# Context columns made by VectorE's 32x32 transposes, with permuted query weights and 512-wide column tiles

## The chip, the cores and the metric

One core of a Trainium2 chip runs the whole program. The metric is the device time of one execution in microseconds, the median of several runs. TensorE (PE, with its weight loads as PEld), VectorE (DVE), ScalarE (ACT), GpSimd (POOL) and SyncE (SP, which here only issues transfers) each work through their own instruction queue in order and wait for one another by semaphores.

## The reference, cut to what matters

Eight examples, 64 slots of width 512 each, attend three times to a context of 1601 rows of width 512; then follow self-attention and a mixture of experts over the slots, which the change leaves alone. All is fp32.

```python
Pn = rmsnorm(P, input_norm_w)                 # P: 8 x 1601 x 512
k_proj, v_proj = Pn @ Wk.T, Pn @ Wv.T
for _ in range(3):
    sn = rmsnorm(slots, slot_norm_w)
    scores = einsum('bkd,bmd->bkm', sn @ Wq.T, k_proj) * SCALE
    attn = softmax(scores, axis=-2)           # over the 64 slots
    attn = attn / (sum(attn, axis=-1) + EPS)  # over the 1601 rows
    updates = einsum('bkm,bmd->bkd', attn, v_proj)
    slots = gru_cell(updates, slots, ...)
```

`rmsnorm` divides each context row by the root of its mean square, so that the sum of squares of every row is needed once.

## The kernel before, in words

The projections are folded: Wq and Wk become one matrix `wqk` (scaled by the slot norm's weights; the input norm's weights are applied to the query as `qscale`), and Wv is folded into the recurrent weights as `wvi`. So the scores are a product of the query with the raw context, and the context is needed in two layouts: with the 512 features on partitions ("columns", for the scores) and with the rows on partitions (for the weighted sum).

Two examples form a pair t, and there are four pairs. Each pair has three iterations, each of two halves: X makes the query and the scores and the softmax (`attend`, L335), Y makes the weighted sum and the recurrent cell (`update`, L423). Pairs 0 and 2 lead, pairs 1 and 3 trail by one iteration, so the halves of two pairs lie in turn (`stages`, L199 to L204).

In the first X of a pair, `prepare` (L270) makes the columns. The context comes in chunks of 1 MB, four rows of 512 features to a partition (`pn_X`), and a tail of 65 rows per example. For each 128 rows ACT squares the tile and sums the squares (L286, into `junk`), TensorE turns it in four 128x128 transposes (`transpose4`, L110, into PSUM tiles `tr_p`), and DVE and ACT in turn copy the result out (`evacuate`, L84 and L86) into a column tile `pT_a`. Column tiles hold 384 columns, the fourth 449. Each finished tile is also stored to DRAM (`kept`, issued by POOL at L294) and loaded again by the second and third iteration (`pT_X`). From the sums of squares, thirteen small DVE instructions (from L298 on) make the reciprocal roots `inv` and the roots `rms`, which the softmax uses.

`attend` turns the slots (`sT`), multiplies by `wqk` (`pq`), copies and turns the query (`qT`, DVE at L354) and multiplies it by the columns, group by group (`sc`, L364). ACT scales the scores out of PSUM (L370). Softmax then runs on blocks of 512 (L395 to L402 on DVE, exp on ACT), with POOL making row sums (`part`, L404 to L410). `update` reads the context rows (`pn_Y`), multiplies (`pu`, L433), and goes through the recurrent matmuls (L153) and the gate arithmetic on DVE and ACT (L459 to L470).

What sets the order: all context loads go through SP's queue in the order of the program (`queue`, L116). Chunks of rows have five slots (`nat`), column tiles five (`ctxT`), tails two; `pump` (L242) issues the next planned load as soon as a slot of its kind is counted free by `done` (L254). The other instructions are ordered per engine by a planner at compile time, which follows the program's priorities and its own estimates of when operands are ready; the order is then fixed. In the first X, the chunks are made inside `attend` through `start_group` (L489), between the folds of the value weights (`fold_values`). In the other first X's the whole of `prepare` stands ahead of `attend` in the program.

Of the kernel before, what the change touches and what calls it, by code (L numbers as in the profile page):

```python
# [9 lines left out]
F32 = mybir.dt.float32  # L10
I32 = mybir.dt.int32
AF = mybir.ActivationFunctionType
ALU = mybir.AluOpType
# [18 lines left out]
RSQRT_SEED = 0x5F3759DF  # L32


GROUPS = ((0, 384), (384, 768), (768, 1152), (1152, M))
GW = max(hi - lo for lo, hi in GROUPS)


@with_exitstack
def perceiver_kernel(  # L40
# [26 lines left out]
    def chunk(name, tag="w"):  # L67

        bufs, width = SLOTS[tag]
        return big.tile([P, width], F32, tag=tag, name=name, bufs=bufs)  # L70
# [4 lines left out]
    def bank(name, tag="ring"):  # L75
        return ps.tile([P, 512], F32, tag=tag, name=name)
# [3 lines left out]
    def evacuate(dst, src):  # L80

        copies[0] += 1
        if copies[0] % 2:
            nc.vector.tensor_copy(dst, src)  # L84
        else:
            nc.scalar.copy(dst, src)  # L86
# [19 lines left out]
    def transpose4(src, name, rows=P, tag="ring"):  # L106

        pt = bank(f"tr_{name}", tag).rearrange("p (c m) -> p c m", c=DC)
        for c in range(DC):
            nc.tensor.transpose(pt[:, c, :rows], src[:rows, ts(c, P)], ident[:rows, :rows])  # L110
        return pt[:, :, :rows]
# [4 lines left out]
    def queue(dst, src):  # L116

        return tc.keep_in_program_order(nc.sync.dma_start(dst, src))  # L118
# [11 lines left out]
        queue(wk_s[:, c, :], wk[ts(c, P), :])  # L130
    snw_s = const.tile([P, DC], F32, name="snw_s")
    inw_s = const.tile([P, DC], F32, name="inw_s")
    with nc.allow_non_contiguous_dma(reason="two short vectors onto partitions"):
        nc.gpsimd.dma_start(snw_s, snw.rearrange("(c p) -> p c", p=P))
        nc.gpsimd.dma_start(inw_s, inw.rearrange("(c p) -> p c", p=P))
    queue(xall, x.rearrange("(t p) d -> p t d", p=P))
    qscale = const.tile([P, DC], F32, name="qscale")
    nc.vector.tensor_scalar_mul(qscale, inw_s, float(D) ** -0.5)
    rw_s = const.tile([P, DC, E], F32, name="rw_s")
    nc.gpsimd.dma_start(rw_s, rw.rearrange("(c p) e -> p c e", p=P))  # L140

# [42 lines left out]

    mv0, r0 = layernorm(xall, "in", NPAIR)


    kept = [
        [
# [15 lines left out]

    tiles = {}
    held = {"nat": 0, "tail": 0, "ctxT": 0}
    plan = {"nat": [], "tail": [], "ctxT": []}  # L210
    BUFS = {"nat": SLOTS["nat"][0], "tail": 2, "ctxT": SLOTS["ctxT"][0]}
    for pos, (half, (t, it)) in enumerate(stages):
        if half == "Y" or it == 0:
            for k in range(3):
                for j in range(2):
                    plan["nat"].append((pos, ("row", half, t, it, j, k)))
            for j in range(2):
                plan["tail"].append((pos, ("row", half, t, it, j, 3)))
        if half == "X":
            for g in range(len(GROUPS)):  # L220
                for j in range(2):
                    plan["ctxT"].append((pos, ("col" if it else "made", half, t, it, j, g)))

    def load(key):
        kind, half, t, it, j, k = key
        b, name = 2 * t + j, f"{2 * t + j}_{k}_{half}{it}"
        if kind == "col":
            lo, hi = GROUPS[k]
            ct = chunk(f"pT_{name}", "ctxT")[:, : DC * (hi - lo)]
            queue(ct, kept[b][k])  # L230
            tiles[key] = ct.rearrange("p (c m) -> p c m", c=DC)
        elif k < 3:
            c = chunk(f"pn_{name}", "nat").rearrange("p (a f) -> p a f", a=4)
            src = ctxp[b, : MT * P, :].rearrange("(p i) d -> p i d", i=MT)
            queue(c, src[:, 4 * k : 4 * k + 4, :])
            tiles[key] = c
        else:
            tl = big.tile([P, D], F32, tag="tail", name=f"tail_{name}", bufs=BUFS["tail"])
            queue(tl[:TAIL], ctxp[b, MT * P :, :])
            tiles[key] = tl  # L240
# [13 lines left out]
    def done(tag, n=1):  # L254

        held[tag] -= n
        pump()

    def row_tile(half, t, it, j, i):

        c = tiles[("row", half, t, it, j, i // 4)]
        return c[:, i % 4, :] if i < MT else c[:TAIL]

    def row_used(i):
        if i % 4 == 3:
            done("nat")
        elif i == MT:
            done("tail")

    def prepare(t):  # L270

        ss = small.tile([P, NMT, 2], F32, tag="pss", name=f"pss_{t}", bufs=4)
        nc.gpsimd.memset(ss, 0.0)
        for g, (lo, hi) in enumerate(GROUPS):
            for j in range(2):
                b = 2 * t + j
                key = plan["ctxT"].pop(0)[1]
                assert key == ("made", "X", t, 0, j, g)
                held["ctxT"] += 1
                ct = chunk(f"pT_{b}_{g}_a", "ctxT")[:, : DC * (hi - lo)]  # L280
                c3 = ct.rearrange("p (c m) -> p c m", c=DC)
                for i in range(lo // P, (hi + P - 1) // P):
                    src = row_tile("X", t, 0, j, i)
                    k = src.shape[0]
                    junk = work.tile([P, D], F32, tag="junk", name=f"junk_{b}_{i}")
                    nc.scalar.activation(  # L286
                        junk[:k], src, AF.Square, accum_out=ss[:k, i, j : j + 1]
                    )
                    evacuate(
                        c3[:, :, i * P - lo : i * P - lo + k],  # L290
                        transpose4(src, f"p_{b}_{i}", k, "gate"),
                    )
                    row_used(i)
                nc.gpsimd.dma_start(kept[b][g], ct)  # L294
                tiles[key] = c3
            yield g
        v = small.tile([P, NMT, 2], F32, tag="pv", name=f"pv_{t}", bufs=2)
        nc.vector.tensor_scalar(v, ss, 1.0 / D, 1e-6, ALU.mult, ALU.add)  # L298
        ri = const.tile([P, NMT, 2], F32, name=f"inv_{t}")
        flat = "p i j -> p (i j)"  # L300
        rsqrt(ri.rearrange(flat), v.rearrange(flat), 2 * NMT, f"p_{t}")
        rms = const.tile([P, NMT, 2], F32, name=f"rms_{t}")
        nc.vector.tensor_mul(rms, v, ri)
        inv_of[t], rms_of[t] = ri, rms
# [17 lines left out]
        wih_2.append(w)  # L322
    wqk = chunk3("wqk")
    for dc in range(DC):
        if dc % 2:
            nc.vector.tensor_scalar_mul(wqk[:, dc, :], pw[dc], snw_s[:, dc : dc + 1])
        else:
            nc.scalar.mul(wqk[:, dc, :], pw[dc], snw_s[:, dc : dc + 1])
    b_h = work.tile([P, NMT * P], F32, tag="wide", name="b_h", bufs=3)[:, : 2 * D]
    nc.gpsimd.dma_start(b_h, bhh[: 2 * D].partition_broadcast(P))  # L330
    nc.vector.tensor_add(b_i[:, : 2 * D], b_i[:, : 2 * D], b_h)
# [3 lines left out]
    def attend(t, it, first=lambda g: None):  # L335
# [4 lines left out]
        nc.vector.tensor_copy(sT, transpose4(slots, f"s_{n}"))  # L340
        sT_of[t] = sT
        ss = small.tile([P, 1], F32, tag="sss", name=f"sss_{n}")
        junk = work.tile([P, D], F32, tag="junk", name=f"junk_{n}")
        nc.scalar.activation(junk, slots, AF.Square, accum_out=ss)
        nc.vector.tensor_scalar(ss, ss, 1.0 / D, 1e-6, ALU.mult, ALU.add)
        ri = small.tile([P, 1], F32, tag="sri", name=f"sri_{n}")

        pq = bank(f"pq_{n}")
        matmul4(pq, lambda c: sT[:, c, :], lambda c: wqk[:, c, :])
        q = work.tile([P, D], F32, tag="nat", name=f"q_{n}", bufs=2)  # L350
        nc.scalar.copy(q, pq)
        rsqrt(ri, ss, 1, f"s_{n}")
        qT = work.tile([P, DC, P], F32, tag="quT", name=f"qT_{n}", bufs=2)
# [4 lines left out]
        for g, (lo, hi) in enumerate(GROUPS):  # L358
            first(g)
            sc = bank(f"sc_{n}_{g}")[:, : hi - lo]  # L360
            cols = [tiles[("col" if it else "made", "X", t, it, j, g)] for j in range(2)]
            for c in range(DC):
                for j in range(2):
                    nc.tensor.matmul(  # L364
                        sc[j * S : (j + 1) * S, :],
                        lhsT=qT[:, c, ts(j, S)], rhs=cols[j][:, c, :],
                        start=c == 0, stop=c == DC - 1,
                    )
            done("ctxT", 2)
            nc.scalar.mul(raw[:, lo:hi], sc, ri)  # L370

        e = work.tile([P, NMT * P], F32, tag="wide", name=f"e_{n}", bufs=3)
# [50 lines left out]
    def update(t, it, att, banks=None):  # L423
# [6 lines left out]
        for i in range(NMT):  # L430
            k = P if i < MT else TAIL
            for j in range(2):
                nc.tensor.matmul(  # L433
                    pu[j * S : (j + 1) * S, :],
                    lhsT=e[:k, i, ts(j, S)], rhs=row_tile("Y", t, it, j, i),
                    start=i == 0, stop=i == MT,
                )
                row_used(i)
# [87 lines left out]
    NI = 8  # L526
    A = 4
    scale = float(HD) ** -0.5
    bq_n = work.tile([P, DX], F32, tag="junk", name="bq_n")[: 3 * HEADS, :P]
    bq_n = bq_n.rearrange("n (q c) -> n q c", q=4)  # L530
    for q in range(4):
        queue(bq_n[:, q, :], bqkv.rearrange("(n c) -> n c", c=HD))
# [199 lines left out]

    xbuf = dram.tile([NB * P, DX], F32, name="xbuf")
    back = dram.tile([TOP * NPAIR * P, D], F32, name="back")
    zeros = work.tile([P, DX], F32, tag="junk", name="zeros")
    nc.gpsimd.memset(zeros, 0.0)
    nc.gpsimd.memset(zeros[:, D : D + 1].bitcast(I32), TOP * NPAIR * P)
    tc.keep_in_program_order(nc.gpsimd.dma_start(
# [306 lines left out]
```

## Time and profile before

| what | value |
| --- | --- |
| device time, median of 3 runs | 1056.72 us (1051.85 to 1061.62) |
| the profiled execution: device time, span | 1067.05 us, 1065.3 us |
| mean granted TensorE clock | 0.969 |
| context chunks `pn_X` loaded by SP | 24 of 1 MB |
| column tiles stored, and loaded again | 32, 64 |
| DMA, mean over the span | 223 GB/s |

A line of groups has the source line, the engine, the operation, the tiles written and read, the partitions and elements, the number of instructions; then their busy time, the mean time of one in ns; then the idle time of the engine just before them and what ended most of it. A line of a stretch of time has busy times and instruction counts of the engines in it. Overlapping instructions of one engine count once in busy times.

### The profile page before, as it was taken

What the parts mean: (1) busy time and instruction counts of PE and PEld (TensorE: products, weight loads), DVE (VectorE), ACT (ScalarE), POOL (GpSimd) and SP (SyncE); (2) the same over time, 40 slices, a digit from 0 to 9 for tenths busy, and PEclk for the clock granted to TensorE, in tenths of its full rate; (3) what the DMA queues carried; (4) which work ended last, traced back from release to release, by engine and by line L of the source; (5) the groups of instructions that cost most, each with busy time, mean ns of one, the idle gap of its engine ahead of it and who ended that gap; (6) DMA issues with size and microseconds to landing.
All of it is one profiled execution on the core that took longest, in us unless ns stands there. A gap on an engine that the chain in (4) does not pass through costs nothing. (4 is left out here: it accounts for less than half of the span.)

```text
span 1065.3 us, 11266 instructions
## 1 busy us (share of the span) xinstructions
PE 971.7 (91%) x4081; PEld 461.3 (43%) x4081; DVE 428.6 (40%) x1059; ACT 246.7 (23%) x530; POOL 198.0 (19%) x295
## 2 busy tenths in 40 slices
PE   6899989899989997999898899899998988899994
PEld 3454354334433444444543344333443464675441
DVE  3224155532544347522554224452451445542223
ACT  1652552110211524205521001110110111211220
POOL 2003013300133004300132100330051211031221
PEclk9999999999999998999899999999999969999998
DMA  9946678864656647845787564596191300039943
GB/s 344 400 135 274 249 296 347 317 255 168 246 232 263 246 136 270 316 151 214 306 336 270 223 247 186 197 357 247 59 348 40 129 2 0 1 134 309 371 158 136
DMA packets 62425, 237.41 MB, mean 223 GB/s; under 512 B 5870, under 2 KB 20222, under 8 KB 50080
## 3 DMA queue, kind: packets, MB, share of 16 engines
q1 hardware_dynamic: 52576, 195.44, 48.6%
q0 software_dynamic: 8640, 39.14, 9.4%
q10 hardware_dynamic: 1152, 2.10, 0.5%
q8 instruction: 33, 0.54, 0.2%
q14 instruction: 24, 0.20, 0.0%
HBM read 201.22 MB, written 36.48 MB: 223 GB/s over the span
## 5 line engine op out<-in xcount | busy, mean ns | idle before, releaser
L433 PE MATMUL pu<-pn_Y,e 128*64 128x512 f32 x576 | 144.1, 609 | 5.7 <-DMA pn_Y<-in_ctxp 5.7
L364 PE MATMUL sc<-pT_X,qT 128*64 128x384 f32 (+1 forms) x512 | 102.4, 505 | 11.7 <-DMA pT_X<-kept 7.4
L404 POOL TENSOR_TENSOR raw<-e,rms 128x512 f32<-128x512 f32 (+1 forms) x48 | 44.8, 936 | 275.4 <-DVE sm L400 153.1
L433 PEld LDWEIGHTS pu<-pn_Y,e 128*64 128x64 f32 x576 | 42.3, 139 | 95.7 <-issue 79.6
L286 ACT ACTIVATE junk<-pn_X 128x512 f32<-128x512 f32 x96 | 60.4, 629 | 40.9 <-DMA pn_X<-in_ctxp 38.6
L364 PEld LDWEIGHTS sc<-pT_X,qT 128*64 128x64 f32 x512 | 38.1, 136 | 70.2 <-issue 47.8
L110 PE MATMUL tr_p<-ident,pn_X 128*128 128x128 f32 x384 | 53.4, 290 | 14.0 <-DMA pn_X<-in_ctxp 8.8
L395 DVE TENSOR_REDUCE mx<-tr_e 128x8 f32<-128x512 f32 (+1 forms) x48 | 26.9, 581 | 97.4 <-PE tr_e L384 97.3
L294 POOL DMA_DIRECT2D kept<-pT_a x32 | 17.4, 545 | 214.3 <-ACT r L467 66.3
L84 DVE COPY pT_a<-tr_p 128x512 f32<-128x512 f32 x52 | 34.7, 685 | 53.1 <-PE tr_p L110 31.8
L110 PEld LDWEIGHTS tr_p<-ident,pn_X 128*128 128x128 f32 x384 | 44.4, 147 | 26.9 <-issue 14.6
L370 ACT ACTIVATE raw<-sc,sri 128x384 f32<-128x384 f32 (+1 forms) x48 | 28.6, 596 | 107.8 <-PE sc L364 107.6
L153 PE MATMUL pq<-wqk,sT 128*128 128x512 f32 x96 | 48.0, 646 | 4.9 <-DVE sT L340 3.9
L153 PE MATMUL pr<-wvi,uT 128*128 128x512 f32 x96 | 45.5, 617 | 4.1 <-DVE uT L450 3.9
L398 ACT ACTIVATE e<-e 128x512 f32<-128x512 f32 (+1 forms) x48 | 25.8, 547 | 98.9 <-DVE e L397 98.8
L364 PE MATMUL sc<-pT_a,qT 128*64 128x384 f32 (+1 forms) x256 | 46.2, 503 | 2.4 <-DVE qT L354 2.4
L153 PE MATMUL pr<-whh,sT 128*128 128x512 f32 x96 | 48.1, 612 | 0.0
L153 PE MATMUL pqkv<-wqkv,haT 128*128 128x512 f32 x96 | 44.2, 618 | 1.4 <-ACT haT L549 1.4
L153 PE MATMUL pz<-whh,sT 128*128 128x512 f32 x96 | 44.7, 597 | 0.0
L153 PE MATMUL pab<-up_b,xT 128*128 128x512 f32 x96 | 43.2, 594 | 0.8 <-ACT xT L86 0.7
L153 PE MATMUL phn<-whh,sT 128*128 128x512 f32 x96 | 43.5, 592 | 0.0
L153 PE MATMUL pz<-wvi,uT 128*128 128x512 f32 x96 | 43.2, 592 | 0.0
(240 smaller groups left out, 1348.1 us busy)
## 6 DMA issues: line engine op xcount, KB each, us to landing
pn_Y<-in_ctxp SPq DMA_DIRECT2D x72, 1024.0 KB
pT_X<-kept SPq DMA_DIRECT2D x48, 768.0 KB
pn_X<-in_ctxp SPq DMA_DIRECT2D x24, 1024.0 KB
kept<-pT_a POOLq DMA_DIRECT2D x24, 768.0 KB, 8.6
pT_X<-kept SPq DMA_DIRECT2D x16, 898.0 KB
up_b<-in_w SPq DMA_DIRECT2D x24, 512.0 KB
kept<-pT_a POOLq DMA_DIRECT2D x8, 898.0 KB, 10.1
dn_b<-in_w SPq DMA_DIRECT2D x12, 512.0 KB
```

What stands on the lines that cost most here:

```text
L84: nc.vector.tensor_copy(dst, src)
L110: nc.tensor.transpose(pt[:, c, :rows], src[:rows, ts(c, P)], ident[:rows, :rows])
L153: nc.tensor.matmul(dst, lhsT=lhsT(c), rhs=rhs(c), start=start and c == 0, stop=stop and c == DC - 1,)
L286: nc.scalar.activation(junk[:k], src, AF.Square, accum_out=ss[:k, i, j : j + 1])
L294: nc.gpsimd.dma_start(kept[b][g], ct)
L364: nc.tensor.matmul(sc[j * S : (j + 1) * S, :], lhsT=qT[:, c, ts(j, S)], rhs=cols[j][:, c, :], start=c == 0, stop=c == DC - 1,)
L370: nc.scalar.mul(raw[:, lo:hi], sc, ri)
L395: nc.vector.reduce_max(mxr, rows3(pt), axis=AX.X)
L398: nc.scalar.activation(ee, ee, AF.Exp)
L404: nc.gpsimd.tensor_mul(rows3(prod), ee, wide(rms))
L433: nc.tensor.matmul(pu[j * S : (j + 1) * S, :], lhsT=e[:k, i, ts(j, S)], rhs=row_tile("Y", t, it, j, i), start=i == 0, stop=i == MT,)
```

## The change

The chunk loads of the first pass put the data so that DVE's 32x32 transposes are enough. A chunk is now 512 consecutive rows. Partition quadrant a (32 partitions) receives features 128a to 128a+127 of all 512 rows, in four transfers per chunk, one for each quadrant, in runs of 128 floats. Each partition then holds 16 runs of 128 features. Four DVE stream transposes of 128x512 turn every 32x32 block in place of its quadrant, straight from the chunk to the column tile. A feature that was on partition p of feature chunk c is now somewhere else, in blocks of 32: so `wqk`'s columns are written permuted (`by_block`), and the input norm's weights are loaded a second time in that order (`inw_b`) for `qscale`. Column tiles hold 512 columns; the tail of 65 rows has column tiles of its own (`tailT`, two slots), and is still turned by TensorE after POOL has permuted its features.

The sums of squares change with the layout. ACT squares the whole chunk in place after the transposes (128x2048), POOL adds 128 features down to 32 in two instructions (1024 and 512 elements), DVE reduces the 32. A row's sum then lies in four parts on four quadrants; TensorE adds these with a constant matrix (`fold`), four small matmuls for each pair, and DVE copies the result. The chunk's slot is released after the reduction. The scores read the columns with a pattern of 32-element blocks. The tile `junk` is gone; three other uses of it move to other tiles (`q`, `part`, and for the zeros stored to `xbuf` a weight slot).

```diff
-GROUPS = ((0, 384), (384, 768), (768, 1152), (1152, M))
-GW = max(hi - lo for lo, hi in GROUPS)
+KT = 4
+NK = MT // KT
+GW = KT * P
+Q = 32
+GROUPS = tuple((lo, min(lo + GW, M)) for lo in range(0, M, GW))
...
+        for a in range(P // Q):
+            nc.gpsimd.dma_start(
+                inw_b[ts(a, Q)], inw[ts(a, P)].rearrange("(b c) -> c b", c=Q)
+            )
...
-    nc.vector.tensor_scalar_mul(qscale, inw_s, float(D) ** -0.5)
+    nc.vector.tensor_scalar_mul(qscale, inw_b, float(D) ** -0.5)
...
+    def by_block(v):
+        return v.rearrange("p (a b c) -> p b a c", a=P // Q, c=Q)
...
+    BUFS = {"nat": SLOTS["nat"][0], "tail": 2, "ctxT": SLOTS["ctxT"][0], "tailT": 2}
...
+    def by_chunk(ct, g):
+        if g < NK:
+            return ct.rearrange("p (n b r) -> p b n r", b=DC, r=Q)
+        return ct.rearrange("p (b r) -> p b r", b=DC)
...
-        elif k < 3:
-            c = chunk(f"pn_{name}", "nat").rearrange("p (a f) -> p a f", a=4)
-            src = ctxp[b, : MT * P, :].rearrange("(p i) d -> p i d", i=MT)
-            queue(c, src[:, 4 * k : 4 * k + 4, :])
+        elif k < NK:
+            c = chunk(f"pn_{name}", "nat")
+            src = ctxp[b, ts(k, GW), :]
+            if half == "Y":
+                c = c.rearrange("p (i d) -> p i d", i=KT)
+                queue(c, src.rearrange("(p i) d -> p i d", i=KT))
+            else:
+                src = src.rearrange("(q r i) d -> r i q d", q=P // Q, r=Q)
+                for a in (0, 2, 1, 3):
+                    dst = c[ts(a, Q)].rearrange("r (i q d) -> r i q d", i=KT, d=P)
+                    queue(dst, src[:, :, :, ts(a, P)])
...
     def prepare(t):
-        ss = small.tile([P, NMT, 2], F32, tag="pss", name=f"pss_{t}", bufs=4)
+        ss = small.tile([P, NK, 2, KT, P // Q], F32, tag="pss", name=f"pss_{t}", bufs=1)
...
-                for i in range(lo // P, (hi + P - 1) // P):
-                    src = row_tile("X", t, 0, j, i)
-                    k = src.shape[0]
-                    junk = work.tile([P, D], F32, tag="junk", name=f"junk_{b}_{i}")
-                    nc.scalar.activation(
-                        junk[:k], src, AF.Square, accum_out=ss[:k, i, j : j + 1]
+                if g < NK:
+                    for i in range(KT):
+                        nc.vector.transpose(ct[:, ts(i, D)], src[:, ts(i, D)])
+                    nc.scalar.activation(src, src, AF.Square)
+                    sq = src.rearrange("p (n d) -> p n d", d=P)
+                    nc.gpsimd.tensor_add(sq[:, :, :64], sq[:, :, :64], sq[:, :, 64:])
+                    nc.gpsimd.tensor_add(sq[:, :, :32], sq[:, :, :32], sq[:, :, 32:64])
+                    nc.vector.reduce_sum(
+                        ss[:, g, j].rearrange("p i q -> p (i q)"), sq[:, :, :32], axis=AX.X
                     )
-                    evacuate(
-                        c3[:, :, i * P - lo : i * P - lo + k],
-                        transpose4(src, f"p_{b}_{i}", k, "gate"),
+                else:
+                    src = src[:TAIL]
+                    blocks = work.tile([P, D], F32, tag="nat", name=f"tailb_{b}", bufs=2)[:TAIL]
+                    nc.gpsimd.tensor_copy(
+                        blocks.rearrange("p (b a c) -> p b a c", b=DC, c=Q), by_block(src)
                     )
-                    row_used(i)
+                    nc.scalar.activation(src, src, AF.Square, accum_out=v[:TAIL, MT, j : j + 1])
+                    evacuate(tiles[key], transpose4(blocks, f"p_{b}", TAIL, "gate"))
                 nc.gpsimd.dma_start(kept[b][g], ct)
+                done("nat" if g < NK else "tail")
             yield g
+        ps4 = bank(f"pss_{t}", "gate")[:, : 2 * MT]
+        for q in range(P // Q):
+            nc.tensor.matmul(
+                ps4[ts(q, Q)], lhsT=fold, rhs=ss[:, :, :, :, q].rearrange("p k j i -> p (k j) i"),
+                start=True, stop=True,
+            )
+        nc.vector.tensor_copy(
+            v[:, :MT].rearrange("p (k i) j -> p k j i", k=NK),
+            ps4.rearrange("p (k j i) -> p k j i", k=NK, j=2),
+        )
...
     for dc in range(DC):
+        src, dst = by_block(pw[dc]), wqk[:, dc, :].rearrange("p (b a c) -> p b a c", b=DC, c=Q)
...
-                        lhsT=qT[:, c, ts(j, S)], rhs=cols[j][:, c, :],
+                        lhsT=qT[:, c, ts(j, S)], rhs=cols[j][:, c],
...
-            done("ctxT", 2)
+            done("ctxT" if g < NK else "tailT", 2)
...
-    zeros = work.tile([P, DX], F32, tag="junk", name="zeros")
+    zeros = chunk("zeros")[:, :DX]
```

## The prediction

> **What bounds the kernel now.** I read the page's first two parts, then the groups, then the same 197 us of the trace twice: busy times of the four stretches in which the context columns are made, once for all instructions and once for the transposes' tile `tr_p` alone. The page first, then a groups answer:
>
> ```profile
> PE 971.7 (91%) x4081; PEld 461.3 (43%) x4081; DVE 428.6 (40%) x1059; ACT 246.7 (23%) x530; POOL 198.0 (19%) x295
> ...
> L110 PE MATMUL tr_p<-ident,pn_X 128*128 128x128 f32 x384 | 53.4, 290 | 14.0 <-DMA pn_X<-in_ctxp 8.8 <-DVE pT_a L84 2.9 <-ACT pT_a L86 1.9
> L86 ACT COPY pT_a<-tr_p 128x512 f32<-128x512 f32 (+1 forms) x52 | 28.4, 554 | 32.1 <-PE tr_p L110 12.4 <-PE sc L364 11.6 <-DVE pT_a L84 7.3
> L84 DVE COPY pT_a<-tr_p 128x512 f32<-128x512 f32 x52 | 34.7, 685 | 53.1 <-PE tr_p L110 31.8 <-PE sc L364 16.6 <-ACT pT_a L86 4.7
> L643 DVE STREAM_TRANSPOSE on<-oT 128x512 f32<-128x512 f32 x4 | 2.7, 695 | 0.0
> ```
>
> TensorE is the bound: 91% busy, the next engine 40%. 53.4 us of it are the transposes that the change removes; the last line is the price of their replacement. The four stretches, all instructions, then `tr_p` alone:
>
> ```profile
> 24.00:86.00 62.00, 58.45 (x256) 32.52 (x257) 16.23 (x41) 33.55 (x80) 4.28 (x8) 0.97 0.75 289
> 124.00:165.00 41.00, 35.31 (x194) 21.03 (x193) 19.44 (x63) 21.47 (x52) 3.80 (x7) 1.00 0.62 243
> 380.00:437.00 57.00, 49.90 (x277) 27.94 (x276) 30.28 (x75) 21.14 (x47) 14.87 (x22) 0.91 0.72 253
> 506.00:543.00 37.00, 32.72 (x191) 20.84 (x190) 15.83 (x57) 17.94 (x41) 4.33 (x8) 0.91 0.82 317
> ```
>
> ```profile
> 24.00:86.00 62.00, 13.85 (x104) 12.30 (x104) 8.88 (x13) 7.16 (x13) 0.97 0.75 289
> 124.00:165.00 41.00, 12.27 (x104) 10.96 (x104) 8.56 (x13) 6.75 (x13) 1.00 0.62 243
> 380.00:437.00 57.00, 15.51 (x104) 11.88 (x104) 8.71 (x13) 7.06 (x13) 0.91 0.72 253
> 506.00:543.00 37.00, 13.11 (x104) 11.63 (x104) 8.56 (x13) 7.11 (x13) 0.91 0.82 317
> ```
>
> Columns after the stretch and its length: PE, PEld, DVE, ACT (in the first table POOL too), clock, DMA share, GB/s. The transposes take 12 to 16 us of each stretch, and PE idles only 3 to 7 us there: PE time removed is time of the stretch, if nothing else is late.
>
> **The parts, from rows.** *PE, removed:* 384 transposes, 53.4 us; the 32 of the two tails per pair stay. With them go waits of up to 14.0 us. *PE, added:* four folds of four small matmuls; a fp32 matmul is two records (the row sums `rs`, 12 in the code, are recorded 24 times), so 32 records at 46 ns (L624: 11.7/256) to 192 ns (L440: 4.6/24), 1.5 to 6.1 us; I take 3. *Scores:* before, 768 records. On PE's timeline 32 of 384 columns take 5.38 us, 168 ns each; 28 of these with 16 of 449 take 7.92 us, so a 449 takes 201 ns. After: 576 of 512 columns at 224 ns (168 scaled) to 250 ns (L433: 144.1/576), 192 of 65 at 46 ns (L624) to 139 ns (53.4/384). Change: 576 x (56 to 82) - 192 x 201 + 192 x (46 to 139) = +2.5 to +35 us; I take 3, since the same line scaled and the row of like size are nearest. That the column operand now comes in blocks of 32 elements has no row on PE; DVE's and ACT's block-wise copies (L638, 411 and 375 ns for 256) cost no more than plain ones (L447, L448: 483 and 474), so 0.
>
> *DVE:* 96 transposes x 0.695 = 66.7 us and 24 row reductions x 0.672 (L399's median) = 16.1 us come; all 52 copies (34.7 us) go and 4 of the tails' eight come back at some 0.4: +50 us, 12.5 a stretch. *ACT:* squares and their accumulator reads (60.4 + 18.0 us) and 48 of 52 copies (27) go; 24 squares of 2048 come, 1.6 us each by the slope from 256 to 512 elements (474 to 630 ns) to 2.5 us as four of 0.63: at 2.0, some -57 us. *POOL:* 24 x two adds of 1024 and 512 elements; 128, 256 and 512 take 0.45, 0.74 and 1.04 us (medians of L410, L406, L404), so 1.6 to 2.1 and 1.04: +70 us, 17 a stretch. ACT and POOL have room: the busiest stretch has 21 and 15 us of 57.
>
> *DMA:* each context megabyte of the first pass comes as four transfers onto 32 partitions in 512-byte runs, not as one in 8 KB runs. SP issues 72 more at 0.33 us, 24 us of an idle queue. At full share the trace moves 412 GB/s in 8 KB runs (162 to 177 us), and 368 GB/s in the experts' 1 and 2 KB runs (970 to 1000 us); 512 bytes are not shown. Bounds per megabyte: 2.5 us at 412, 5.7 us if a packet costs the same whatever its size (half of 368). I take the middle, 4.1: +1.6 us on 24 loads, 38 us. Room: unused DMA share in the four stretches is 62x0.25 + 41x0.38 + 57x0.28 + 37x0.18 = 54 us. It fits on average, but each load lands later.
>
> The Trainium skill speaks against this part (SBUF — State Buffer, section "Door 1: The DMA port swizzle"): 32 partitions reach 8 of 16 ports, 189 GB/s at 1 MiB against 328. As an estimate from its ratio, a megabyte would take 4.4 us, and the 24 loads 45 us more instead of 38. No transfer of before shows it.
>
> *At nothing:* four more short loads for `inw_b` on POOL at 0.82 us each delay its other loads by 3.3 us; the first read of these is at 23.9 us. The zeros in a weight slot that comes free only with the last update (829 us) are needed at 947. `junk` in place: ACT's own order. Six column tiles in five slots, where there were eight in five, can only shorten the 7.4 us that scores wait for `pT_X`; not counted.
>
> **What is kept of it on the path, by stretch.**
> First: SP has 12 transfers, not 3, ahead of wih_1; six chunks at +1.6 us land up to 10 us later. DVE's `wqk` (L326, at 30.75 us) stands behind context copies already and will stand behind transposes that wait for a slower load; behind it PE waits for `sT`. Of 13.85 I keep 7.
> Second and fourth: from 135.5 us, and the same after 507, PE ran 60 transposes while nothing else was released; DVE was busy 2.0 of 25 us just before (100 to 125), so columns can be made then, under the update's matmuls. I keep 12.3 + 13.1 + their waits for `pn_X` (2.4 + 1.9) = 29.7.
> Third: DVE runs almost without a gap from 395.8 to 417.7, softmax and column copies mixed, and `sT` of the next query (413.0 us) stands behind them. DVE's extra 12.3 us lie in just this queue. Of 15.5 and some 4.6 us of waits for copies I keep 20.1 - 12.3 = 7.8.
> Together 44.5. Off: folds 3, scores 3, and the new wait. The sum of squares of the last chunk now goes transposes, square (2.0), adds (2.9), reduction (0.7), fold: 5.6 us in which PE's fold, if it stands ahead of scores or `tr_e`, holds all behind it. Scores cover it in part; I take a quarter, 1.4 x 4 = 5.6. **Sum: 33 us saved.** The profiled execution took 1067.05 us (span 1065.3), 1.0% above the median of 1056.72; subtracted from that: **1024 us**.
>
> New waits and what stands behind them: DVE's reduction waits for POOL, and behind it stand `upd`, `uT`, `qT` and the gate arithmetic, for which PE waits; ACT's square waits for four transposes, with exp and tanh behind it; POOL's adds wait for ACT, with `kept` stores and the row sums behind.
>
> **Rivals.**
> *All of it is kept* (1000 us or less): DVE finds gaps everywhere and the tail hides; 53.4 + 14.0 - 6 = 61, so 996. For: DVE 40%. Against: third stretch.
> *Given back, no change* (about 1056): late context transfers and DVE's queue take PE's place in all four. At 5.7 us a megabyte six loads need 34 us, of stretches 37 to 62 us long that PE would leave 12 us shorter. For: DMA share 0.72 to 0.82 in the last two. Against: loads are issued 20 to 35 us ahead (347 and 476 us). Here belongs that PE work leaves without the program getting shorter.
> *Slower* (1076): DVE's in-order queue. Were each reduction to stand right behind its own transposes, DVE would stand still 2.0 + 2.9 = 4.9 us for each of 24 chunks, 118 us, beside waits for the slower loads. Where less than 28% of this (33/118) reaches PE the change still wins; at 45%, 53 us, it is 20 us slower. For: ACT, whose queue holds the squares now, waited 38.6 us for `pn_X`, where little depended on it; on DVE much does. The two engines also hinder each other: L406 on POOL takes 717, 744 (median) and 1726 ns. Against: order in the program is arranged by expected readiness; `wqk` and the copies of before are interleaved, not in the order written.
>
> **How the numbers follow.** Forecast 0.46 (1008 to 1045); all kept 0.13; given back 0.14; slower 0.27, of it a few hundredths for transfers alone. Within 1% (10.6 us) is about what a measurement of this kernel can't tell from no change: its three runs span 1051.85 to 1061.62. Faster by more: 0.46 + 0.13 = 0.59; same 0.14; slower 0.27. The range reaches from the upper part of "all kept" (1000) to a slower case of +22 us (1079).
>
> **What would show it.** Right: `tr_p` down to 32 records and PE near 925 us busy; 96 DVE stream transposes near 0.7 us; DVE near 480, ACT near 190, POOL near 270 us; PE's idle time in the stretches not above 30 us; the third gaining least. Wrong: DVE waiting tens of us for POOL sums or for `pn_X`; PE waiting for `qT`, `uT`, `pT_a` or the fold; a megabyte of 512-byte runs above 5 us; 65-column scores near 139 ns; transposes from SBUF slowed by POOL beside them.

## The result, and the profile after

The changed kernel takes **1150.51 us** (median; 1147.5 to 1153.92) against 1059.17 us of the kernel before in the same comparison: a ratio of 1.089, interval 1.082 to 1.096. It is slower by 91 us. The forecast was 1024 us.

The first part of the page of the changed kernel and two rows of its second part (busy tenths of PE, and the clock granted to it, in 40 slices of the span):

```profile
PE 941.2 (82%) x3729; PEld 418.2 (36%) x3729; DVE 475.1 (41%) x1135; ACT 198.0 (17%) x314; POOL 292.2 (25%) x360
...
PE   5399935789988994599828889988998888898994
...
PEclk9599976999999997799859999999998899999998
```

TensorE is still the busiest engine, but it now idles 1152.1 - 941.2 = 211 us of the span (94 before), and its clock falls where it idles. The groups of the same page that stand where the transposes and their copies stood:

```profile
L330 DVE STREAM_TRANSPOSE pT_a<-pn_X 128x512 f32<-128x512 f32 x96 | 59.9, 679 | 18.4 <-PE sc L425 16.4
L333 POOL TENSOR_TENSOR pn_X<-pn_X 128x1024 f32<-128x1024 f32 x24 | 56.5, 2355 | 40.5 <-ACT pn_X L331 35.6
L331 ACT ACTIVATE pn_X<-pn_X 128x2048 f32<-128x2048 f32 x24 | 45.8, 1908 | 105.4 <-DVE pT_a L330 105.3
...
L335 DVE TENSOR_REDUCE pss<-pn_X 128x16 f32<-128x512 f32 x24 | 16.4, 683 | 97.8 <-POOL pn_X L334 97.8
...
L113 PE MATMUL tr_p<-ident,tailb 65*128 65x65 f32 x32 | 5.2, 329 | 56.8 <-POOL tailb L341 56.8
```

The new work costs about what it was priced at (the second number after the bar is the mean in ns); only GpSimd's adds are longer. What was not priced is the third number, the idle time in front of it: VectorE stands 97.8 us for GpSimd's sums, ScalarE 105 us for VectorE's transposes, and TensorE 56.8 us for the permuted copy of the tail.

Where in the program is the time lost? TensorE turns the update (`tr_u`) at the same points of the work in both kernels. I cut both spans there: the stretches of one row hold the same work. Columns as before (stretch, length, PE, PEld, DVE, ACT, POOL busy, clock, DMA share, GB/s). The kernel before, the second, fourth and fifth of six stretches:

```profile
124.00:218.00 94.00, 82.38 (x395) 41.49 (x393) 48.80 (x125) 30.28 (x68) 24.25 (x34) 1.00 0.74 294
...
331.00:461.00 130.00, 122.25 (x504) 56.93 (x505) 58.48 (x138) 41.35 (x96) 24.59 (x35) 0.96 0.65 243
461.00:597.00 136.00, 121.94 (x504) 57.10 (x502) 58.02 (x143) 41.52 (x95) 25.48 (x35) 0.96 0.66 257
```

The changed kernel, the same three:

```profile
136.00:259.00 123.00, 78.95 (x312) 33.15 (x310) 60.77 (x144) 26.23 (x37) 47.48 (x49) 0.83 0.74 262
...
375.00:520.00 145.00, 111.36 (x413) 44.93 (x413) 72.76 (x157) 28.83 (x42) 46.15 (x49) 0.88 0.62 191
520.00:676.00 156.00, 115.90 (x416) 47.20 (x414) 68.84 (x162) 28.42 (x40) 48.97 (x49) 0.87 0.74 242
```

They last 29, 15 and 20 us longer; the first stretch (0 to 124, now 0 to 136) 12 us, the third 3, the rest 8. So most of the loss, 76 of 87 us of span, lies where columns are made. In the stretch of 123 us TensorE has 83 instructions less, yet is busy only 3.4 us less, with the clock at 0.83 there and 1.00 before, and idles 44 us instead of 12.

The timeline of that stretch shows how. VectorE of the changed kernel (start, length, instruction, and in brackets the idle time before it and what ended it):

```profile
159.90 0.69 DVE L335 TENSOR_REDUCE pss<-pn_X 128x16 f32<-128x512 f32 x1 [5.28 <-POOL pn_X L334]
160.50 2.48 DVE L330 STREAM_TRANSPOSE pT_a<-pn_X 128x512 f32<-128x512 f32 x4
168.84 0.69 DVE L335 TENSOR_REDUCE pss<-pn_X 128x16 f32<-128x512 f32 x1 [5.85 <-POOL pn_X L334]
169.44 2.48 DVE L330 STREAM_TRANSPOSE pT_a<-pn_X 128x512 f32<-128x512 f32 x4
177.77 0.69 DVE L335 TENSOR_REDUCE pss<-pn_X 128x16 f32<-128x512 f32 x1 [5.85 <-POOL pn_X L334]
```

Each reduction stands right behind the transposes of its own chunk, and the next chunk's transposes behind that (in the whole span VectorE waits so 20 times for 24 chunks): 2.48 us of transposes, 5.85 of standing, 0.69 of reduction, 8.9 us per chunk, from one start to the next, of which VectorE works 3.2. TensorE beside it:

```profile
148.36 0.60 PE L113 MATMUL tr_s<-ident,slots 128*128 128x128 f32 x4
149.90 3.70 PE L161 MATMUL pq<-wqk,sT 128*128 128x512 f32 x8 [0.94 <-DVE sT L402]
178.34 1.25 PE L113 MATMUL tr_p<-ident,tailb 65*128 65x65 f32 x8 [24.74 <-POOL tailb L341]
184.20 1.11 PE L113 MATMUL tr_q<-ident,q 128*128 128x128 f32 x4 [4.61 <-ACT q L412]
```

Behind the query's `pq` stand the tail's transposes. GpSimd permutes the tail at 177.68, behind the adds of the fourth chunk, so TensorE does nothing for 24.7 us; then `q` comes late, because ScalarE's copy of it (183.57) stands behind the square of one more chunk (180.88).

### The profile page after: what moved, and what is told of

Same layout as the page of the kernel before. It is cut to its first block, busy times and chain, and to the rows that moved or that the text cites. A ratio compares the mean times of both kernels' runs of the same rounds, so it can differ in the third digit from the quotient of the medians.

```text
span 1152.1 us, 10618 instructions
## 1 busy us (share of the span) xinstructions
PE 941.2 (82%) x3729; PEld 418.2 (36%) x3729; DVE 475.1 (41%) x1135; ACT 198.0 (17%) x314; POOL 292.2 (25%) x360
## 5 line engine op out<-in xcount | busy, mean ns | idle before, releaser
L425 PE MATMUL sc<-pT_X,qT 128*64 128x512 f32 (+1 forms) x512 | 98.3, 512 | 6.4 <-DVE qT L415 4.4
L161 PE MATMUL pq<-wqk,sT 128*128 128x512 f32 x96 | 55.5, 732 | 35.7 <-DVE sT L402 20.8
L330 DVE STREAM_TRANSPOSE pT_a<-pn_X 128x512 f32<-128x512 f32 x96 | 59.9, 679 | 18.4 <-PE sc L425 16.4
L333 POOL TENSOR_TENSOR pn_X<-pn_X 128x1024 f32<-128x1024 f32 x24 | 56.5, 2355 | 40.5 <-ACT pn_X L331 35.6
L331 ACT ACTIVATE pn_X<-pn_X 128x2048 f32<-128x2048 f32 x24 | 45.8, 1908 | 105.4 <-DVE pT_a L330 105.3
L335 DVE TENSOR_REDUCE pss<-pn_X 128x16 f32<-128x512 f32 x24 | 16.4, 683 | 97.8 <-POOL pn_X L334 97.8
L425 PE MATMUL sc<-pT_a,qT 128*64 128x512 f32 (+1 forms) x256 | 51.4, 543 | 2.4 <-DVE sss L407 1.6
L113 PE MATMUL tr_p<-ident,tailb 65*128 65x65 f32 x32 | 5.2, 329 | 56.8 <-POOL tailb L341 56.8
L431 ACT ACTIVATE raw<-sc,sri 128x512 f32<-128x512 f32 (+1 forms) x48 | 27.6, 595 | 125.8 <-PE sc L425 101.9
L161 PEld LDWEIGHTS pq<-wqk,sT 128*128 128x128 f32 x96 | 22.0, 239 | 66.1 <-issue 29.1
L161 PE MATMUL pz<-whh,sT 128*128 128x512 f32 x96 | 44.5, 594 | 0.0
```

The lines of the kernel that those rows point to most:

```text
L161: nc.tensor.matmul(dst, lhsT=lhsT(c), rhs=rhs(c), start=start and c == 0, stop=stop and c == DC - 1,)
L330: nc.vector.transpose(ct[:, ts(i, D)], src[:, ts(i, D)])
L331: nc.scalar.activation(src, src, AF.Square)
L333: nc.gpsimd.tensor_add(sq[:, :, :64], sq[:, :, :64], sq[:, :, 64:])
L335: nc.vector.reduce_sum(ss[:, g, j].rearrange("p i q -> p (i q)"), sq[:, :, :32], axis=AX.X)
L425: nc.tensor.matmul(sc[j * S : (j + 1) * S, :], lhsT=qT[:, c, ts(j, S)], rhs=cols[j][:, c], start=c == 0, stop=c == DC - 1,)
```

## The experiments

**Undoing the standing in the queues, one at a time.** `e1_order` moves each reduction two chunks later in VectorE's order:

```diff
+LAG = 2
...
-                    nc.vector.reduce_sum(
-                        ss[:, g, j].rearrange("p i q -> p (i q)"), sq[:, :, :32], axis=AX.X
-                    )
+                    late.append((g, j, sq))
+                    if len(late) > LAG:
+                        reduce_one()
```

> Edit: each chunk's reduction is put on DVE's queue behind the transposes of the second chunk after it; all the same instructions. Theory A (DVE stands behind each reduction for ACT's square and POOL's adds, 97.8 us in all, so that a chunk costs 8.9 us in series): DVE's wait for POOL falls below 30 us, the tail's copy on POOL is reached earlier, and the time falls from 1150 to 1040 to 1080. Theory B (PE's wait for the tail's permuting copy on POOL, 56.8 us, is its own fault): POOL's work is the same, 3.6 us a chunk with the copy in the same place behind four of them, PE still waits 40 us or more: 1120 to 1150. Theory C (the 512-byte loads arrive too slowly): chunks come no faster, 1130 to 1150.

`e2_tail` lets four loads with runs of 128 bytes permute the tail, in place of GpSimd's `tailb`; `e5_order_tail` does both; `e12_order_tailact` moves the reductions and has ScalarE make the copy of the tail:

```diff
-                    nc.gpsimd.tensor_copy(
+                    nc.scalar.copy(
```

> Edit: the tail of 65 rows is permuted by its load (four transfers in 128-byte runs) instead of by a copy on POOL; nothing else. Theory B: PE's 56.8 us of waiting for the copy go and the time falls by 40 to 57, to 1093 to 1110. Theory A: PE waits for DVE's columns and for the query's copies in DVE's queue instead, the time falls by 20 at most, 1130 to 1150. Theory C: as A.

> Both remedies at once: each reduction two chunks later in VectorE's order, and the tail's features permuted by four loads with runs of 128 bytes instead of GpSimd's copy. Queue theory (the time is lost where VectorE stands for GpSimd's sums and TensorE stands for the tail's permuted copy): alone they gave 23 and 6 us; the waits they remove are 83 of 98 us and 57 us, so together, when neither can hide behind the other, 40 to 60 us less than the changed kernel, 1090 to 1110 us. Load theory (chunks of 512-byte runs come too late whatever stands in the queues): about the sum of the two, 30 us less, 1115 to 1125 us, with VectorE's transposes waiting for pn_X instead (15 us in the run with the order alone).

> Each reduction two chunks later in VectorE's order, GpSimd's adds kept, and the tail's permuted copy on ScalarE instead of GpSimd; all computed. Beside the run with the order and the tail by short loads (1107 us), TensorE no longer waits 20 us for the tail's loads in the first stretch. Queue theory: 1085 to 1105 us. Load theory: the chunks' arrival takes the place of the tail, 1105 to 1115.

| kernel | median us | ratio to before |
| --- | --- | --- |
| changed | 1150.5 | 1.089 (1.082 to 1.096) |
| `e1_order` | 1127.1 | 1.062 (1.056 to 1.068) |
| `e2_tail` | 1144.5 | 1.077 (1.071 to 1.083) |
| `e5_order_tail` | 1106.9 | 1.044 (1.038 to 1.050) |
| `e12_order_tailact` | 1108.3 | 1.045 (1.041 to 1.049) |

The order gives 23 us, the tail 6, both 44: each alone leaves the other wait in its place. `e1_order` lies far above the 1040 to 1080 us that the queue theory gave it, `e12_order_tailact` in the 1105 to 1115 of the load theory. Two of the many waits of TensorE and VectorE in `e1_order` (a line has who waited, for whom, then us in total, times, longest):

```profile
PE tr_p L114 <- POOL tailb L351: 38.2, 5, 15.4
...
DVE pss L323 <- POOL pn_X L344: 15.0, 4, 4.7
```

VectorE's standing is down from 97.8 to 15 us, 83 us less, and the time by 23 us, 28% of that. In `e2_tail` the tail's wait is gone from GpSimd and TensorE waits 32.7 us for the columns (`sc` for `pT_a`) and 39.7 us for `sT`, both behind VectorE, and 20 us for the tail's slow loads. 48 us of loss remain with both undone.

**The loads and the sums, each taken away.** `e3_nosums` leaves out the chunks' squares, adds and reductions. `e4_contig` loads a chunk of the first pass by one transfer in 8 KB runs. `e9_nosums_contig` does both. `e7_before_quad` is the kernel before with nothing but the quadrant loads. `e6_contig_tr` is `e4_contig` with VectorE held to transposes, reduction, transposes, reduction. `e8_nosums_tail` is `e3_nosums` with the tail permuted by loads. In all but `e3_nosums` and `e8_nosums_tail` the features then lie where the rest of the program does not expect them; without the sums a constant stands for them.

```diff
-                for a in (0, 2, 1, 3):
-                    dst = c[ts(a, Q)].rearrange("r (i q d) -> r i q d", i=KT, d=P)
-                    queue(dst, src[:, :, :, ts(a, P)])
+                queue(c.rearrange("p (i d) -> p i d", i=KT), src.rearrange("(p i) d -> p i d", i=KT))
```

> Edit: the sums of squares of the chunks are left out (square, both adds, reduction), and a constant stands for them; the tail's stay. Theory A: nothing stands between transposes, 1010 to 1045, at or below the forecast of 1024. Theory B: POOL's queue is empty ahead of the copy, so as A. Theory C: the loads still set the pace, 1090 or more.

> Edit: each first-pass chunk is loaded by one transfer in 8 KB runs instead of four in 512-byte runs; the features are then not where the scores expect them. Theory C: a megabyte takes 2.5 us instead of 4.5, the time falls by 50 or more, below 1100. Theory A: chunks had arrived when their turn came in all but one case (DVE waited 1.9 us for them), only the first stretch gains, 5 to 20 us: 1130 to 1145. Theory B: as A.

> The chunks of the first pass come by one transfer each in 8 KB runs, as in the kernel before (so the features do not lie where the query expects them), but VectorE's order is held as transposes, reduction, transposes, reduction. The run with such loads and a free order took 1080 us. Load theory: the load itself is what costs, so this stays near it, 1080 to 1095 us. Queue theory: the free order was the gain, the loads only led the planner to it, so this loses most of it again, 1115 to 1145 us, with 70 to 100 us of VectorE's reductions waiting for GpSimd.

> The kernel before with nothing changed but the chunk loads of the first pass: four transfers onto 32 partitions each, in 512-byte runs, as in the changed kernel (the rows and features are not where the rest expects them). The loads alone: 24 MB at 4.5 instead of 2.5 us/MB are 48 us of transfer time. Load theory: 35 to 70 us slower than before (1095 to 1130), with TensorE's tr_p waiting tens of us for pn_X. Queue theory: the loads hide as my prediction had it, 0 to 20 us slower (1060 to 1080).

> Chunk sums of squares left out (a constant stands for them) and the tail permuted by the load: with neither of the two queues' waits only the loads and the columns are left. The run without the sums took 1064 us, with 38 us of TensorE waiting for the tail's copy on GpSimd. Queue theory: another 15 to 35 us go, 1030 to 1050 us, which is faster than before and near what I had forecast for the whole change. Load theory: the wait passes to the loads (sc and tr_p behind pn_X and the tail), 1055 to 1065 us.

> Neither the chunk sums (a constant in their place) nor the quadrant loads (one transfer of 8 KB runs per chunk; the features do not lie where the query expects them): what is left is TensorE without its 384 transposes against VectorE's 96. If TensorE's time leaves the span as my prediction had it, 44 to 61 us of the span of before go: 1000 to 1020 us. If removed TensorE time mostly turns into waiting whatever the loads and sums do, it stays above 1040. The two costs measured one by one, 86 us for the sums and 13 (with the order held) to 21 us (on the kernel before) for the loads, give 1150 - 86 - 17 = about 1045.

| kernel | median us | ratio to before |
| --- | --- | --- |
| `e3_nosums` | 1064.2 | 1.004 (1.001 to 1.007) |
| `e4_contig` | 1079.8 | 1.017 (1.012 to 1.023) |
| `e6_contig_tr` | 1137.9 | 1.075 (1.069 to 1.080) |
| `e7_before_quad` | 1081.1 | 1.020 (1.014 to 1.027) |
| `e8_nosums_tail` | 1076.1 | 1.015 (1.009 to 1.021) |
| `e9_nosums_contig` | 1034.8 | 0.977 (0.972 to 0.981) |

Three things follow. *First,* with neither sums nor quadrant loads the change would be worth 24 us. This is what TensorE's removed transposes bring, together with whatever the sums cost in the kernel before, which makes them on ScalarE (60.4 us of squares); no run leaves them out there. *Second,* the loads cost 29 us there (1034.8 to 1064.2), and 22 us put on the kernel before. *Third,* making the sums costs 86 us (1064.2 to 1150.5). That -24 + 29 + 86 = 91 is no proof, since each run is the next one's base, and the shares depend on the order of the steps: by way of `e4_contig` the sums cost 45 us (1034.8 to 1079.8) and the loads 71 (1079.8 to 1150.5). So sums and loads are not separate costs; 86 and 29 are one way of dividing 116 us.

The tail shows how they meet. TensorE waits 37.6 us for the tail's copy in `e3_nosums`, where GpSimd adds no squares, and 8.6 us in `e9_nosums_contig`. In the first stretch (17.6 and 8.6 us) the tail's load goes out behind the chunks' loads, at 31.3 and 15.6 us. In the fourth stretch of the changed kernel (375 to 520 us) the copy stands behind the other pair's row sums on GpSimd, and TensorE's 11.79 us there are 11.78 in `e3_nosums`. So of the 56.8 us only a part is due to the adds.

In `e7_before_quad` the loads' cost is no single wait: of TensorE's 16.4 us in front of `tr_p`, 7.7 are for `pn_X`. `e6_contig_tr` shows that the gain of 71 us in `e4_contig` is mostly not the faster load but the order. With the fast load the transposes of three chunks stand ahead of the first reduction in the first stretch, and VectorE's wait for sums is 41.3 us in all. Held to the order of the changed kernel, with the same fast load, it is

```profile
DVE pss L325 <- POOL pn_X L348: 107.0, 22, 6.7
```

and 58 of the 71 us are lost again: with this order the fast load is worth 13 us. That the planner arranges it so because it expects the four transfers late fits these two runs; its reckoning isn't in any trace. In `e8_nosums_tail` the miss of my expectation is the tail's own load: TensorE waits 21.4 us for it, 19.2 at once in the first stretch, where it comes behind twelve chunk transfers.

**What in the sums costs?** Two other ways of making the sums come first. `e10_pool_sums` lets GpSimd add down to one value, so that VectorE waits for no sum (the tail's copy on ScalarE). `e11_dve_sum` drops GpSimd's adds and has VectorE reduce all 2048 squares:

```diff
-                    nc.gpsimd.tensor_add(sq[:, :, :64], sq[:, :, :64], sq[:, :, 64:])
-                    nc.gpsimd.tensor_add(sq[:, :, :32], sq[:, :, :32], sq[:, :, 32:64])
                     nc.vector.reduce_sum(
-                        ss[:, g, j].rearrange("p i q -> p (i q)"), sq[:, :, :32], axis=AX.X
+                        ss[:, g, j].rearrange("p i q -> p (i q)"), sq, axis=AX.X
```

> GpSimd adds all the way down (five more adds of 256 to 16 elements per chunk), so that VectorE has no instruction that waits for a sum; the tail's permuted copy goes to ScalarE, away from GpSimd's queue. The result is complete. Queue theory: nearly all of what the run without the sums gained comes back, 1065 to 1090 us; GpSimd gets some 60 us more work in which row sums of the softmax wait. Work theory (the sums cost because of the work itself, wherever it stands): 1110 to 1140 us.

> GpSimd's two adds are taken out of the chain and VectorE reduces all 2048 squares of a partition itself, right behind its transposes as before. Per chunk VectorE stands about 1.9 us for ScalarE's square instead of 5.5 us for square and adds, and works some 1.5 to 2 us more: the chain of 8.9 us per chunk becomes 6.5 to 7. Queue theory: 24 x about 2 us and the tail's wait on GpSimd (57 us of TensorE, which then stands behind no adds) shrink; half to all of it reaches the end: 1090 to 1125 us. Work theory (VectorE's load is what counts): 40 us more work on VectorE make it no faster, 1150 or more.

They took 1126.0 us (ratio 1.062, 1.057 to 1.066) and 1131.3 us (1.065, 1.059 to 1.070). Both fell short of what my theory of VectorE's queue gave them (1065 to 1090 and 1090 to 1125). In `e11_dve_sum` VectorE still stands 44.3 us for the squares. In `e10_pool_sums` no reduction of VectorE waits for GpSimd any more, but its copy of the folds waits 35.5 us for TensorE, which waits for GpSimd's sums, and for other in-order queues (`e10_pool_sums`, the longest waits of TensorE):

```profile
PE tr_p L113 <- ACT tailb L344: 19.5, 8, 8.4
PE pss L354 <- POOL pss L337: 19.3, 4, 8.5
PE pq L161 <- DVE sT L405: 18.1, 6, 4.6
PE tr_s L113 <- ACT wqk L393: 16.9, 1, 16.9
PE pq L161 <- DVE sri L93: 14.1, 1, 14.1
PE tr_q L113 <- ACT q L415: 12.4, 9, 3.7
```

So another rival: the sums come too *late*, and the softmax waits for the last of them. `e13_unused` is the changed kernel, `e14_order_unused` is `e12_order_tailact`, and in both all sums are made, but the folds read a constant. `e15_late_fold` is `e12_order_tailact` with the fold and the roots put behind the scores in the program.

```diff
-                ps4[ts(q, Q)], lhsT=fold, rhs=ss[:, :, :, :, q].rearrange("p k j i -> p (k j) i"),
+                ps4[ts(q, Q)], lhsT=fold, rhs=given,
```

> The changed kernel with all its squares, adds and reductions in place, but the folds read a constant: the softmax's roots no longer wait for the sums (the result is not complete for that reason). Standing theory (the sums cost because VectorE, and behind it the transposes and copies, stand for GpSimd): VectorE's order and its some 98 us of waiting stay, so this stays at 1120 to 1150 us. Lateness theory (the sums cost because the last of them comes after the scores, and the roots, the scaling of the scores and the softmax come behind it): 1065 to 1095 us, near the run that makes no sums at all (1064).

> As the run with the reductions two chunks later and the tail's copy on ScalarE (1108 us), but the folds read a constant, so that nothing of the softmax waits for a sum. All the work of the sums is still done on ScalarE, GpSimd and VectorE. Lateness theory: what was left of the loss beyond the loads was the lateness of the last sum, 1065 to 1080 us. Standing theory: work in the queues and held slots are what is left, 1095 to 1110 us.

> As the run with the reductions two chunks later and the tail's copy on ScalarE (1108 us), all computed, but the fold and the roots made from it stand in the program behind the scores instead of ahead of them, so that the query's own root (sri), for which ScalarE's scaling of the scores waited 8 and more us a stretch, does not stand behind the last sum in VectorE's queue. Lateness theory: 5 to 9 us in each of the three later stretches come back, 1080 to 1095 us. Standing theory: 1100 to 1112 us.

1144.0 us (1.079, 1.069 to 1.090), 1112.4 (1.048, 1.040 to 1.056) and 1096.5 (1.032, 1.024 to 1.040). With nothing waiting for the sums the time is what it was, within 7 us: lateness is at most a small part. The test is not clean, since in both runs VectorE is busy 21 to 22 us longer (see the last section). That the fold behind the scores gives 12 us all the same I put down to the order it leads to, which no run here separates from lateness. It is the best of the complete versions, and still slower than before.

Left were the chunk's slot, held until the reduction, and the work itself in the queues. `e16_hold` is `e14_order_unused` without squares and adds, and with a copy of 16 elements in place of each reduction, two chunks late, so that the slot stays held. `e17_late_contig` is `e15_late_fold` with the loads in 8 KB runs.

> As the run with the reductions late and unused (1112 us), but ScalarE's squares and GpSimd's adds are left out and a copy of 16 elements stands in place of each reduction (constants stand for the sums): the chunk's slot is still held until two chunks later, and the work on ScalarE and GpSimd is gone. If the loss is in the slots held (later loads), 1095 to 1112 us. If it is in the squares and adds standing in the queues ahead of the query's and the tail's copies, it comes back to the run without sums: 1062 to 1075.

> The best of the complete versions (reductions two chunks later, tail's copy on ScalarE, fold behind the scores: 1096 us), with the first pass's chunks loaded by one transfer of 8 KB runs (the features do not lie where the query expects them). If the quadrant loads cost what they did without the sums (29 us) whatever stands in the queues, 1062 to 1072 us. If with the queues mended the loads are what is left of the loss, and their lateness was also behind the standing squares, 1040 to 1058.

`e16_hold` takes 1070.7 us (1.013, 1.007 to 1.020): 42 us less than the run that does the work, and 6 above `e3_nosums`, which neither does it nor holds the slot (and has the tail's copy on GpSimd). So in this order 42 us are the cost of the squares, adds and reductions themselves, and held slots are at most a small part. TensorE's waits name what stands behind that work, first in `e14_order_unused`, then in `e16_hold`:

```profile
PE pq L162 <- DVE sT L419: 34.9, 7, 14.5
PE tr_p L114 <- ACT tailb L354: 21.6, 8, 9.0
PE tr_s L114 <- ACT wqk L407: 19.2, 1, 19.2
```

```profile
PE tr_p L114 <- ACT tailb L351: 24.9, 5, 18.5
PE pq L162 <- DVE sT L416: 10.2, 5, 3.9
PE tr_s L114 <- ACT wqk L404: 1.2, 1, 1.2
```

The waits for `sT` and `wqk` fall by 25 and 18 us, that for the tail does not: in the first stretch `wqk` comes 18 us earlier, and TensorE then waits 18.5 us for the tail, whose load sets the pace (its transposes begin at 42.3 us in both). How the cost divides among the three queues, and between standing in a queue and the engines' hindering each other, stays open. `e17_late_contig` takes 1055.3 us (0.998, 0.994 to 1.002): with the order mended the loads are worth 41 us, more than the 29 without sums and less than the 71 between the changed kernel and `e4_contig`, and the change with both would just break even.

## Why the prediction was wrong

- **What bounds the kernel** held as a reading, but "PE time removed is time of the stretch" did not. In `e9_nosums_contig`, without the sums and the slow loads, TensorE's busy time is 55.4 us less (971.7 to 916.3) and the time only 24 us less; I kept 44.5. There TensorE waits 20.2 us for `sT` (3.9 before) and 13.2 us for `pn_Y` (5.7 before).
- **The durations** held: 96 transposes of 679 ns (695 forecast), reductions 683 (672), squares 1.91 us (2.0), VectorE 475 us busy (480), `tr_p` 32 records, folds 1.1 us (3), scores 149.7 us against 148.6 (+3 forecast). GpSimd's adds were too low: 2.36 and 1.29 us (1.6 to 2.1 and 1.04), GpSimd +94 us instead of +70.
- **DMA:** 20 transfers, 5 MB, go out back to back in 22.57 us at 117.4: 4.5 us per megabyte; 4.1 were taken. My estimate of 4.4 from the ratio in the Trainium skill (SBUF — State Buffer, section "Door 1: The DMA port swizzle") is nearer, and the run agrees with it. The mis-sized terms lay behind that. "24 us of an idle queue" was no free queue: SP's line for the first twelve transfers is 24.91 us long (three took 8.67 before), and `wih` behind them starts at 32.81 us instead of 16.84. I took 6.85 of 13.85 us off in the first stretch for all this, and nothing elsewhere; the loads cost 22 us on the kernel before and 29 and more in the changed one.
- **At nothing:** the step misses GpSimd's `tailb` altogether. I wrote that the 32 transposes of the tails stay, and did not ask who now feeds them. The wait for it is TensorE's largest, 56.8 us.
- **The new wait**, 1.4 x 4 = 5.6 us, is the step that failed most: with the folds it stood for what the sums cost beyond busy time, and making them costs 86 us with the slow loads, 45 with the fast ones. I priced the last chunk's way to the fold. What costs is every chunk's sums, as work in front of other work (42 us between `e14_order_unused` and `e16_hold`). I listed what stands behind the waiting instructions on three engines ("`upd`, `uT`, `qT`", "exp and tanh", "`kept` stores and the row sums") and gave these no price.
- **The rival "slower"** had the order right: each reduction stands behind its own transposes, 97.8 us of standing (118 forecast). Its counter-argument, that the order follows expected readiness, was worth nothing as evidence against: the order does change with the load (`e4_contig`), and with the slow loads this very order came out. Its price was wrong too. Undone alone, VectorE's standing returns 28% of itself, just the share at which by my own rule the change breaks even. The other 63 us of the sums' cost are not in this one mechanism: mending the tail's copy on GpSimd too brings 20 us more, and moving the sums off VectorE altogether leaves TensorE waiting for ScalarE and GpSimd. With 91 us against this rival's 20 it was no full account either.
- **The range** took the cases as alternatives. Late loads and standing queues came together, and they act on each other: the loads are worth 29 us without the sums, and with them 13 with VectorE's order held, 41 with it mended, 71 with it left free.

## What to carry to other kernels

When a change moves work from the bound engine into a chain over three others, price for each link what stands behind it in that engine's queue, not the busy time alone: here VectorE was at 41% after 46 us of new work, and no engine but TensorE was busier, yet making the sums cost 45 to 86 us, and TensorE's waits name the small copies behind them (`sT`, `wqk`, `q`, the tail). Follow also the work that the change leaves alone (the tail) back to its new producer. A slower transfer can cost twice, by its own lateness and by the order that comes out with it; try it alone on the old kernel first (`e7_before_quad`).

## What the hardware showed that was not expected

**Idle TensorE makes its remaining work slower.** `e9_nosums_contig` and the changed kernel have the same number of TensorE instructions:

```profile
PE 916.3 (89%) x3729; PEld 409.9 (40%) x3729; DVE 450.5 (44%) x1111; ACT 154.0 (15%) x290; POOL 208.1 (20%) x316
```

The changed kernel is busy 24.9 us longer with them (941.2), at a mean granted clock of 0.915 against 0.964. In the timeline above four 128x128 transposes take 0.60 us in a busy stretch and 1.11 after the wait. So some of the loss is waiting paid a second time. The Trainium skill (TensorE: Matmul & The Clock Gate, section "What's actually happening") says that the clock is halved after an idle window of some 3.4 us; a `pq` matmul of the changed kernel that takes 592 ns at least and 1223 at most agrees with half, and the window's length no run here shows.

**GpSimd's adds hold small VectorE instructions.** In `e14_order_unused` the roots' arithmetic falls beside the adds. VectorE and then GpSimd:

```profile
162.34 1.13 DVE L97 TENSOR_SCALAR inv<-inv 128x26 int32<-128x26 int32 x1
163.50 2.88 DVE L102 TENSOR_TENSOR newton_p<-inv 128x26 f32<-128x26 f32 x1
```

```profile
163.97 2.36 POOL L346 TENSOR_TENSOR pn_X<-pn_X 128x1024 f32<-128x1024 f32 x1
```

The multiplication (`newton_p`) has a median of 186 ns; here it ends 0.05 us after the add. VectorE's busy time is 21 us above that of `e12_order_tailact` (496.8 against 475.6) for the same 1135 instructions, and in `e13_unused` 22 us above the changed kernel's (497.2 against 475.1). This may be part of why taking the dependence away gained nothing; no run separates it. The Trainium skill (SBUF — State Buffer, section "Who interferes with whom") says that a VectorE instruction with two inputs in SBUF and a GpSimd instruction that reads it exclude one another, and the transposes agree: with one input they took 680 ns on average in this run and 679 in `e3_nosums`, which has no adds of squares. One input is not always enough, though: the TENSOR_SCALAR shown, with one, took 1.13 us and in the first stretch 2.28, against 0.18 in `e12_order_tailact`.
